# Re-planning the last stretch of a 145-step kernel: half ticks, fixed places, and an earlier fetch

## The chip, the cores and the metric

The kernel runs on one core of a Trainium2 chip. TensorE does matrix products and transposes, VectorE and ScalarE do element-wise work, GpSimd does a power and issues accumulating transfers, and SyncE issues almost all other transfers. The metric is the time of one execution in microseconds (us), as the median over runs.

## The reference

The input `x` has 32 images of 14 x 14 pixels and 512 channels, in float32. Two layers follow each other; both normalise in 32 groups of 16 channels first and both add their input back.

```python
for i in range(18):                                   # layer 0, on gn(x)
    nx = gelu(x @ block_w[i] + block_b[i])            # 512 x 512, every pixel
    if i in (11, 14, 17):
        h = gelu(nx.mean(pixels) @ fc1_w[t] + fc1_b[t])          # 512 -> 128
        gates = softmax((h @ fc2_w[t] + fc2_b[t]).reshape(B, 3, C), axis=1)
        nx = nx + gammas[t] * sum_a(gates[:, a] * anchor[a])     # anchors: x after 1, 4, 9
    x = nx
x = x_in + x                                          # end of layer 0
x = x + conv3x3(gn(x), W, groups=32)                  # layer 1
```

## The kernel before

**Layer 0.** The images are worked on in 8 pairs of tiles (pair 0 to 7; a tile is two images, so a pair is four). Channels lie on the 128 partitions in 4 chunks. One step is one block (`block`, L369) for one pair; 144 blocks and one gap step are interleaved in a written-out order (`steps`, L93 to L104), so that two pairs alternate and TensorE always has products. A block is seven products; after each of them the function `run` (L134) issues whatever stands in a calendar for that **tick**. A block thus has 7 ticks, of 8 matrix instructions (2.63 us) each. `tend` (L107) is the tick after the last block; this text calls it T, and writes T+3 for the third tick behind it. From T on there are no products: a tick is only what the calendar holds, and all engines work through their own queues in the order in which the calendar issues.

**The calendar.** `at` (L115) puts a function at a fixed tick. `put` (L124) looks for the first tick from a wished one on that has enough room left on VectorE ("dve") or ScalarE ("act"); the room of a tick is in `ROOM` (L111) for the blocks and in `TAIL` (L112) behind T. `hold` (L121) takes room away. Functions of one tick are issued in the order in which they were planned. So the calendar decides the order of instructions on each engine, not their times.

**The end of a pair.** After block 17, `plan_head` (L610) plans `gate_hidden` (L500: 4 products `hps` and a gelu), four `gate_base` (L564) on VectorE, `gate_logits` (L515: products `lps`) and `gate_softmax` (L525). `plan_gates` (L630) plans for each channel chunk `gate_part` (VectorE), `gate_last` (ScalarE) and `gate_add` (VectorE). `residual` (L662) adds the kernel's input to the result by an accumulating transfer from GpSimd's queue. `plan_norm` (L704) plans the statistics of layer 1's group norm: `stats`, then three steps `scales_mean` (L208: products `mps` and four small VectorE instructions), `scales_rstd` (L218: products `vps`, one VectorE instruction, a power on GpSimd) and `scales_newton` (L225: five VectorE instructions). `columns` (L669) then writes the un-normalised (e = 0) and normalised (e = 1) values in another order into `xc`, and two transfers from SyncE's queue put each `xc` into a DRAM buffer `x2d`, in runs of 56 numbers (224 bytes). For the last pair the chunks are planned one after the other, and e = 1 is made on VectorE; for the others on ScalarE.

**Layer 1** works in 4 batches of 8 images (two pairs each) and in 16 units per batch, four per channel chunk. `unit_load` (L811) fetches 448 KB from `x2d`; `unit_taps` (L828, tile `cps`) does 6 products, which the profile shows as 12 matrix instructions; `unit_sum` (L843) adds the taps to the un-normalised values on VectorE; `unit_out` (L850, tile `tpo`) transposes the sum on TensorE, and ScalarE copies it out. Every fourth unit a transfer of 784 KB takes a chunk to the output. `plan_unit` (L879) plans one unit. The first three batches fill gaps between blocks; the last six units of batch 2 ("late units", `NLATE` = 6) and all 16 units of batch 3 run behind T. Those 16 need both last pairs' `x2d`, chunk by chunk. There are 5 buffers for a unit's input.

`load_gates` (L471) fetches `fc1_w` (256 KB) and `fc2_w` (512 KB) for a gated block; SyncE's queue issues it in calendar order, between the other transfers.

Of the kernel before, what the change touches and what calls it, by code (L numbers as in the profile page):

```python
# [19 lines left out]
def kernel(  # L20
# [72 lines left out]
    steps = [(0, i) for i in range(12)]  # L93
# [12 lines left out]
    NP7 = 7  # L106
    tend = NP7 * len(steps)  # L107
# [1 line left out]


    ROOM = {"dve": (1.7, 0.0, 3.4, 3.4, 1.7, 0.0, 0.0), "act": (1.0, 0.8, 1.5, 1.5, 1.0, 0.8, 0.8)}  # L111
    TAIL = {"dve": 3.0, "act": 3.6}  # L112
    left = {e: {} for e in ROOM}

    def at(tick, fn, *args):  # L115
        calendar[tick].append((fn, args))

    def room(e, tick):
        return left[e].get(tick, ROOM[e][tick % NP7] if tick < tend else TAIL[e])

    def hold(e, tick, us):  # L121
        left[e][tick] = room(e, tick) - us

    def put(first, need, fn, *args):  # L124

        tick = first
        while any(room(e, tick) < us for e, us in need.items()):
            tick += 1
        for e, us in need.items():
            left[e][tick] = room(e, tick) - us  # L130
        at(tick, fn, *args)
        return tick
# [75 lines left out]
    def scales_mean(d, lo=0, hi=NR):  # L208
        st, mean, dv = d["st"][:, lo:hi], d["mr"][:, 0, lo:hi], d["dv"][:, lo:hi]
        ps = group_sums(f"mps_{d['name']}_{lo}", st[:, :, 1::3], hi - lo)  # L210
        nc.vector.tensor_scalar(mean, ps, 0.5, None, ALU.mult)
        nc.vector.tensor_tensor(
            dv, st[:, :, 1::3], mean.unsqueeze(2).to_broadcast([P, hi - lo, 2]), ALU.subtract
        )
        nc.vector.tensor_mul(dv, dv, dv)
        nc.vector.scalar_tensor_tensor(dv, dv, HW / 2.0, st[:, :, 2::3], ALU.mult, ALU.add)

    def scales_rstd(d, lo=0, hi=NR):  # L218

        ps = group_sums(f"vps_{d['name']}_{lo}", d["dv"][:, lo:hi], hi - lo)  # L220
        ve = d["ve"][:, lo:hi]
        nc.vector.tensor_scalar(ve, ps, 1.0 / HW, 1e-5, ALU.mult, ALU.add)
        nc.gpsimd.tensor_tensor(d["y"][:, lo:hi], ve, mhalf[:, lo:hi], ALU.pow)

    def scales_newton(d, lo=0, hi=NR):  # L225
        ve, y, e, mr = d["ve"][:, lo:hi], d["y"][:, lo:hi], d["e"][:, lo:hi], d["mr"]
        nc.vector.tensor_mul(e, y, y)
        nc.vector.tensor_mul(e, e, ve)
        nc.vector.tensor_scalar(e, e, -0.5, 1.5, ALU.mult, ALU.add)
        nc.vector.tensor_mul(mr[:, 1, lo:hi], y, e)  # L230
        nc.vector.scalar_tensor_tensor(
            mr[:, 2, lo:hi], mr[:, 0, lo:hi], -1.0, mr[:, 1, lo:hi], ALU.mult, ALU.mult
        )
# [376 lines left out]
    def plan_head(p, i):  # L610

        k = at_step[p, i]
        t1 = NP7 * (k + 1)
        name = f"{p}_{i}"
        ti = TARGETS.index(i)
        box = boxes[p, i] = {}
        end = k == len(steps) - 1
        if p == 0:
            at(t1 + 1, gate_differences, k, ti)
        at(t1 + (0 if end else 1), gate_hidden, k, ti, name, box)  # L620
        box["base"] = {
            (h, n): put(t1, {"dve": 1.0}, gate_base, p, i, h, n) for h in range(2) for n in range(2)
        }
        a = t1 + (1 if end else 2)
        while room("dve", a) < 2.2:
            a += 1
        at(a, gate_logits, k, name, box)
        return put(a, {"dve": 2.2}, gate_softmax, ti, name, box)
# [75 lines left out]
    def plan_norm(p, d, a, chunks):  # L704

        def stats(n, c, b):
            if "st" not in d:
                d.update(stats_tiles(f"b{p}"))  # L710
            stats_of(d, boxes[p, NB - 1]["nx"][c // NH][n][:, c % NH], c, n, (b,))

        last = a
        for c in chunks:
            for n in range(2):
                for b in range(NI):
                    last = max(last, put(a, {"dve": 0.36}, stats, n, c, b))
        r = chunks[0] * NB4, (chunks[-1] + 1) * NB4
        b = put(last + 1, {"dve": 0.8}, lambda: scales_mean(d, *r))
        b = put(b + 1, {"dve": 0.2}, lambda: scales_rstd(d, *r))  # L720
        b = put(b + 2, {"dve": 0.8}, lambda: scales_newton(d, *r))
        b += 1
        for c in chunks:
            for n in range(2):
                a = put(a, {"act": 0.6}, columns, p, c, n, d, 0)
        out = []
        for c in chunks:
            for n in range(2):
                for i in range(NI):
                    need = {"dve": 0.4} if p == NPAIR - 1 else {"act": 0.5}  # L730
                    b = put(b, need, columns, p, c, n, d, 1, (i,))
            out.append(b)
        return out
# [26 lines left out]
    UC = GP // 2  # L760
# [115 lines left out]

    done = []

    def plan_unit(m, u, tk, ahead, stay=False):  # L879
        b = tk - ahead  # L880
        if not stay and len(done) >= NBW:
            b = max(b, done[-NBW][0])
        if len(done) >= NX:
            b = max(b, done[-NX][1])
        at(b, unit_load, m, u)
        a = max(b + 2, tk)
        while room("dve", a + 1) < 0.65:
            a += 1
        at(a, unit_taps, m, u)
        b = put(a + 1, {"dve": 0.65}, unit_sum, m, u)  # L890
        b = put(b + 1, {"act": 0.9}, unit_out, m, u)
        done.append((a, b))

    def plan_batch(m):


        ready = [max(ended[p][c] for p in range(m * BP, (m + 1) * BP)) for c in range(NCK)]
        if m < NBAT - 1:
            t0 = ready[-1] + 6
            t1 = ended[(m + 2) * BP - 1][-1] if m < NBAT - 2 else NP7 * at_step[NPAIR - 1, GAP] - 9  # L900
            early = NU - (NLATE + NGAP if m == NBAT - 2 else 0)
            for u in range(early):
                plan_unit(m, u, t0 + (t1 - t0) * u // early, 8)
            if m == NBAT - 2:
                for j in range(NGAP):
                    tk = NP7 * at_step[NPAIR - 1, GAP] + NP7 * j // NGAP
                    hold("dve", tk + 1, -0.65)
                    hold("act", tk + 2, -0.9)
                    if j >= NBW:
                        at(tk - 10, load_bands, (early + j,))  # L910
                    plan_unit(m, early + j, tk, 10, j >= NBW)
                for j in range(NLATE):
                    left["dve"][tend + 1 + j] += 0.65
                    left["act"][tend + 2 + j] += 0.9
                    at(tend - 12 + j, load_bands, (early + NGAP + j,))
                    plan_unit(m, early + NGAP + j, tend + j, 12, True)
        else:
            at(tend - 7, load_bands, (0, 1), wpool, "w", [P, NCK, C])
            for j in range(2):
                at(tend - 8, load_bands, (2 + j,), cvpool, "bw")  # L920
            at(tend + 1, load_bands, (4, 5), wpool, "w", [P, NCK, C])
            tk = 0
            for u in range(NU):
                tk = max(tk + 1, ready[u // UC] + 3, tend + NLATE)
                plan_unit(m, u, tk, 3, True)


    for s in range(TS):
# [23 lines left out]
    NGAP, NLATE = 6, 6  # L952
    LEAD = 35
    for k in range(len(steps)):
        p, i = steps[k]
        if i == GAP:
            for tick in range(NP7 * k, NP7 * (k + 1)):
                left["dve"][tick], left["act"][tick] = 2.4, 2.2
            continue
        if k > 0:  # L960
            at(NP7 * (k - 1), load_block, k)
            for tk, j in ((4, 0), (4, 1), (4, 2), (5, 3)) if p == 0 else ((2, 1), (3, 0), (4, 2), (5, 3)):
                at(NP7 * (k - 1) + tk, sums, k, j)
            if p == 0:
                left["dve"][NP7 * (k - 1) + 4] = 0.0
        if i in TARGETS:
            at(NP7 * k + 4, load_gates, k)
            for tk, us in enumerate((0.8, 0.0, 1.5, 1.5, 0.5, 0.0, 0.0)):
                left["act"][NP7 * k + tk] = us
    for j in range(NLATE):  # L970
        left["dve"][tend + 1 + j] = TAIL["dve"] - 0.65
        left["act"][tend + 2 + j] = TAIL["act"] - 1.05
    for j in range(NLATE):
        left["dve"][tend + 1 + j] = TAIL["dve"] - 0.65
        left["act"][tend + 2 + j] = TAIL["act"] - 0.9
    left["act"][tend] = left["act"][tend + 1] = 0.0
    for j in range(NGAP):
        tk = NP7 * at_step[NPAIR - 1, GAP] + NP7 * j // NGAP
        hold("dve", tk + 1, 0.65)
# [14 lines left out]
    b = NP7  # L994
# [45 lines left out]
```

## Time and profile before

| what | value |
| --- | --- |
| median of 5 runs | 2996.19 us (2992.49 to 2999.58) |
| profiled execution, its own time | 2993.2 us |
| its span, first to last instruction | 2991.5 us |
| TensorE matmul busy | 2942.1 us, 98% of the span |
| VectorE busy | 1735.9 us, 58% |
| ScalarE busy | 1455.4 us, 49% |
| GpSimd busy | 77.5 us, 3% |
| moved by the transfers | 465.36 MB, mean 156 GB/s |

The profile is of one execution. Its rows give a start in us from the span's start, a length, the engine, the source line, the operation, and the tile written and the tiles read. A bracket at the end of a row gives idle time of the engine ahead of it and what ended that idle time. Engine names are PE (TensorE), DVE (VectorE), ACT (ScalarE), POOL (GpSimd) and SP (SyncE); a `q` behind a name is the engine's sequencer, which issues transfers. PEclk is the share of the full clock that TensorE was granted. TensorE's matrix instructions overlap, so a row's length is more than its share of the pace; the pace is read from the starts. When a transfer has landed is read from the semaphore updates that the trace records.

The products of the last block end at 2887.6 us in this execution. What lies behind that is the stretch from T on: 104 us, 3.5% of the span.

### The profile page before, as it was taken

Reading aid. Unit: us, or ns where it says so; the run is one execution under the profiler, and the core shown is the slowest. Engines: PE = TensorE matmul, PEld = TensorE weight load, DVE = VectorE, ACT = ScalarE, POOL = GpSimd, SP = SyncE. Lnnn points to the kernel's source line nnn. Section 1 sums busy time; section 2 is a strip of 40 time slices with the busy share of each in tenths; the row PEclk is TensorE's granted clock in tenths of the full one; section 3 lists DMA queues with packets and bytes.
Section 4 is the critical chain, followed back from the end, with each engine's and each line's share of the span. In section 5 each row is a group of like instructions: output and inputs, shape, how many; then the busy total and the mean of one; then the engine's idle time right before and its main releaser. Section 6 shows DMA issues by size and latency. Waiting matters only on the chain.

```text
span 2991.5 us, 31717 instructions
## 1 busy us (share of the span) xinstructions
PE 2942.1 (98%) x10073; PEld 1808.3 (60%) x10073; DVE 1735.9 (58%) x3317; ACT 1455.4 (49%) x3459; POOL 77.5 (3%) x60
## 2 busy tenths in 40 slices
PE   7999999999999999999999999999999999999996
PEld 4555555555565666666666666666666665656666
DVE  5877777655367454663546635566455663545663
ACT  3445445555455454554545544455445554444562
POOL 0000000000000000000000000000000000000010
PEclk9999999999999999999999999999999999999998
DMA  4444445644375445654456544556445653444689
GB/s 154 154 169 134 155 134 169 182 123 123 124 193 158 134 130 161 189 160 131 153 148 187 166 133 139 171 167 174 140 123 174 176 155 119 131 135 117 206 222 212
DMA packets 385743, 465.36 MB, mean 156 GB/s; under 512 B 150715, under 2 KB 213290, under 8 KB 385578
## 3 DMA queue, kind: packets, MB, share of 16 engines
q1 hardware_dynamic: 355178, 436.85, 48.0%
q0 software_dynamic: 4608, 12.85, 2.5%
q10 hardware_dynamic: 25792, 13.65, 1.7%
q8 instruction: 81, 1.33, 0.2%
q14 instruction: 84, 0.69, 0.1%
HBM read 381.48 MB, written 81.79 MB: 155 GB/s over the span
## 4 chain that ended last, share of the span: by engine, by line
PE 97%; DMA 1%; DVE 1%; issue 0%; POOL 0%; ACT 0%; SPq 0%; DVEq 0%
PE x L388 51%; PE z L388 25%; PE y L388 13%; PE cps L836 5%; PE lps L520 1%; PE tpo L860 1%; PE hps L504 1%; PE tpi L258 1%; DMA x<-x2d 0%; DMA w<-in_L_conv_block_w_dram 0%; DMA x2d<-xc 0%; DMA w<-in_L_conv_fc_w_dram 0%; DVE st_a L196 0%; PE mps_a L203 0%; DMA xin<-in_x_dram 0%; PE vps_a L203 0%
## 5 line engine op out<-in xcount | busy, mean ns | idle before, releaser
L388 PE MATMUL x<-t,s 128*128 128x392 f32 x2304 | 810.0, 494 | 0.0
L401 ACT ACTIVATE o<-c,bias 128x392 f32<-128x392 f32 x720 | 440.8, 620 | 661.2 <-DVE c L425 657.9
L388 PEld LDWEIGHTS x<-t,s 128*128 128x128 f32 x2304 | 432.5, 190 | 297.5
L425 DVE TENSOR_TENSOR c<-x,c 128x392 f32<-128x392 f32 x288 | 160.8, 565 | 516.3 <-PE x L388 424.5
L421 ACT COPY c<-x 128x392 f32<-128x392 f32 x576 | 278.9, 484 | 360.5 <-PE x L388 355.5
L388 PE MATMUL z<-t,s 128*128 128x392 f32 x1152 | 403.1, 493 | 0.0
L388 PE MATMUL x<-t,w 128*128 128x392 f32 x1152 | 403.0, 493 | 0.0
L388 PE MATMUL z<-o,s 128*128 128x392 f32 x1088 | 380.9, 493 | 0.0
L388 PE MATMUL y<-o,w 128*128 128x392 f32 x1088 | 380.5, 492 | 0.0
L388 PE MATMUL x<-o,w 128*128 128x392 f32 x1088 | 380.3, 492 | 0.0
L425 DVE TENSOR_TENSOR c<-y,c 128x392 f32<-128x392 f32 x288 | 163.0, 566 | 294.1 <-PE y L388 206.2
L388 PEld LDWEIGHTS x<-t,w 128*128 128x128 f32 x1152 | 217.9, 190 | 156.7
L388 PEld LDWEIGHTS z<-t,s 128*128 128x128 f32 x1152 | 217.0, 190 | 152.2
L367 DVE TENSOR_TENSOR t<-o,o 128x784 f32<-128x784 f32 x272 | 264.1, 971 | 65.4 <-ACT o L401 63.5
L388 PEld LDWEIGHTS x<-o,w 128*128 128x128 f32 x1088 | 206.4, 190 | 147.2
L388 PEld LDWEIGHTS y<-o,w 128*128 128x128 f32 x1088 | 205.1, 190 | 145.6
L388 PEld LDWEIGHTS z<-o,s 128*128 128x128 f32 x1088 | 205.0, 190 | 145.3
L367 DVE TENSOR_TENSOR t<-o,t 128x784 f32<-128x784 f32 x272 | 264.3, 972 | 4.7
L421 ACT COPY c<-z 128x392 f32<-128x392 f32 x288 | 139.5, 484 | 207.2 <-PE z L388 207.0
L425 DVE TENSOR_TENSOR c<-z,c 128x392 f32<-128x392 f32 x288 | 159.2, 564 | 119.0 <-PE z L388 118.1
L408 ACT ACTIVATE o<-c,bias 128x196 f32<-128x196 f32 x288 | 129.4, 450 | 91.2 <-DVE c L425 90.5
L401 ACT ACTIVATE o<-x,bias 128x392 f32<-128x392 f32 x240 | 137.6, 582 | 72.3 <-PE x L388 66.3
(104 smaller groups left out, 2052.1 us busy)
## 6 DMA issues: line engine op xcount, KB each, us to landing
w<-in_L_conv_block_w_dram SPq DMA_DIRECT2D x144, 1024.0 KB
s<-skeep SPq DMA_DIRECT2D x504, 256.0 KB
x2d<-xc SPq DMA_DIRECT2D x128, 224.0 KB
x<-x2d SPq DMA_DIRECT2D x64, 448.0 KB
skeep<-s SPq DMA_DIRECT2D x72, 256.0 KB
bw<-band SPq DMA_DIRECT2D x38, 384.0 KB
xkeep<-xt SPq DMA_DIRECT2D x32, 392.0 KB
o<-xkeep POOLq DMA_DIRECT2D x32, 392.0 KB, 7.6
```

The lines of the kernel that those rows point to most:

```text
L258: nc.tensor.transpose(tp[:, c * TP : (c + 1) * TP], xs[:, c * P : (c + 1) * P], ident[:TP, :TP])
L367: nc.vector.tensor_tensor(t[j], i0, i1, ALU.subtract)
L388: nc.tensor.matmul(acc[d][:, :N], lhsT=lhsT[:, kk, d * P : (d + 1) * P], rhs=rhs[:, kk, :], start=first and kk == 0, stop=kk == NH - 1, sk ...
L401: nc.scalar.activation(o[:, d, :], srcs[d], AF.Gelu_apprx_tanh, bias=bias[:, r : r + 1])
L408: nc.scalar.activation(o[:, d, sl], srcs[d][:, sl], AF.Gelu_apprx_tanh, bias=bias[:, r : r + 1], accum_out=pooled[:, c, m : m + 1],)
L421: nc.scalar.copy(cs[d], acc[d][:, :N])
L425: nc.vector.tensor_tensor(cs[d], acc[d][:, :N], cs[d], ALU.add)
L504: nc.tensor.matmul(hps[:, :NB4], lhsT=w1[:, kk, :], rhs=box["pooled"][:, kk, :], start=(kk == 0), stop=(kk == NCK - 1),)
L520: nc.tensor.matmul(lps[:, m * NB4 : (m + 1) * NB4], lhsT=w2[:, m * P : (m + 1) * P], rhs=h, start=True, stop=True,)
L836: nc.tensor.matmul(pv[:, :, lo:hi], lhsT=d["bw"][:, g, dy], rhs=xv[:, :, lo + dy - 1 : hi + dy - 1], start=j == 0, stop=j == 2, skip_group ...
L860: nc.tensor.transpose(tp[:NV, j * P : (j + 1) * P], d["xs"][:, g, 0, v * NV : (v + 1) * NV], ident)
```

## The change

All of it is in the planning; no instruction's work changes, but their order does.

- A tick behind T has half the room (`TAIL` 3.0 to 1.5 and 3.6 to 1.7).
- In the last head, `gate_logits` is fixed at T+1 and `gate_softmax` at T+3, behind one late unit's taps; before, the planner put both at T+2, behind two.
- The three steps of `plan_norm` go to fixed ticks, whether there is room or not; this holds for all pairs.
- The six late units and the 16 units of batch 3 stand at fixed places two ticks apart: taps at a, sum at a+1, out at a+2, and the next unit's taps at a+2 as well. Before, they were one tick apart and sum and out went where there was room.
- The last `load_gates` moves from tick 4 of the last block to tick 1.
- `unit_load` of batch 3 is planned up to 6 ticks ahead of the taps instead of 3.

```diff
-    TAIL = {"dve": 3.0, "act": 3.6}
+    TAIL = {"dve": 1.5, "act": 1.7}
...
-        a = t1 + (1 if end else 2)
+        if end:
+            at(t1 + 1, gate_logits, k, name, box)
+            at(t1 + 3, gate_softmax, ti, name, box)
+            return t1 + 4
+        a = t1 + 2
         while room("dve", a) < 2.2:
             a += 1
...
-        b = put(last + 1, {"dve": 0.8}, lambda: scales_mean(d, *r))
-        b = put(b + 1, {"dve": 0.2}, lambda: scales_rstd(d, *r))
-        b = put(b + 2, {"dve": 0.8}, lambda: scales_newton(d, *r))
-        b += 1
+        b = last + 1
+        for us, fn, step in (
+            (0.8, scales_mean, 1), (0.2, scales_rstd, 2), (0.8, scales_newton, 1)
+        ):
+            hold("dve", b, us)
+            at(b, fn, d, *r)
+            b += step
...
-    def plan_unit(m, u, tk, ahead, stay=False):
+    def plan_unit(m, u, tk, ahead, stay=False, fixed=False):
...
-        while room("dve", a + 1) < 0.65:
+        while not fixed and room("dve", a + 1) < 0.65:
             a += 1
         at(a, unit_taps, m, u)
-        b = put(a + 1, {"dve": 0.65}, unit_sum, m, u)
-        b = put(b + 1, {"act": 0.9}, unit_out, m, u)
+        if fixed:
+            b = a + 2
+            at(a + 1, unit_sum, m, u)
+            at(b, unit_out, m, u)
+        else:
+            b = put(a + 1, {"dve": 0.65}, unit_sum, m, u)
+            b = put(b + 1, {"act": 0.9}, unit_out, m, u)
         done.append((a, b))
...
                 for j in range(NLATE):
-                    left["dve"][tend + 1 + j] += 0.65
-                    left["act"][tend + 2 + j] += 0.9
                     at(tend - 12 + j, load_bands, (early + NGAP + j,))
-                    plan_unit(m, early + NGAP + j, tend + j, 12, True)
+                    plan_unit(m, early + NGAP + j, tend + 2 * j, 12 + j, True, True)
...
             for u in range(NU):
-                tk = max(tk + 1, ready[u // UC] + 3, tend + NLATE)
-                plan_unit(m, u, tk, 3, True)
+                tk = max(tk + 2, ready[u // UC] + 4, tend + 2 * NLATE)
+                plan_unit(m, u, tk, min(6, tk - ready[u // UC] - 1), True, True)
...
-            at(NP7 * k + 4, load_gates, k)
+            at(NP7 * k + (1 if k == len(steps) - 1 else 4), load_gates, k)
...
-    for j in range(NLATE):
-        left["dve"][tend + 1 + j] = TAIL["dve"] - 0.65
-        left["act"][tend + 2 + j] = TAIL["act"] - 1.05
-    for j in range(NLATE):
-        left["dve"][tend + 1 + j] = TAIL["dve"] - 0.65
-        left["act"][tend + 2 + j] = TAIL["act"] - 0.9
-    left["act"][tend] = left["act"][tend + 1] = 0.0
+        hold("dve", tend + 2 * j + 1, 0.65)
+        hold("act", tend + 2 * j + 2, 0.9)
+    hold("dve", tend, -0.6)
+    hold("dve", tend + 1, -0.3)
+    hold("dve", tend + 3, 0.85)
+    for tick in range(tend, tend + 4):
+        hold("act", tick, room("act", tick))
```

## The prediction, made before the changed kernel was run

> **What bounds the kernel now.** I read the page first.
>
> ```profile
> PE 2942.1 (98%) x10073; PEld 1808.3 (60%) x10073; DVE 1735.9 (58%) x3317; ACT 1455.4 (49%) x3459; POOL 77.5 (3%) x60
> ...
> PE 97%; DMA 1%; DVE 1%; issue 0%; POOL 0%; ACT 0%; SPq 0%; DVEq 0%
> ```
>
> TensorE is busy nearly throughout and carries 97% of the chain that ends last. Only a stretch where it idles can give time back. The view of its waits names such stretches:
>
> ```profile
> PE cps L836 <- DMA x<-x2d: 9.7, 2, 9.0
> ...
> PE hps L504 <- DMA w<-in_L_conv_fc_w_dram: 3.0, 1, 3.0
> ```
>
> Both stand behind T; its other waits are in the first 27 us or behind T too. Between, TensorE waits for nothing, so only a new wait could change the time there. TensorE's timeline behind T:
>
> ```profile
> 2890.63 1.49 PE L504 MATMUL hps<-pool,w 128*128 128x4 f32 x8 [3.04 <-DMA w<-in_L_conv_fc_w_dram]
> 2891.97 7.46 PE L836 MATMUL cps<-x,bq 128*128 128x224 f32 x24
> 2899.27 1.84 PE L520 MATMUL lps<-h,w 128*128 128x4 f32 x16
> ...
> 2938.91 4.05 PE L836 MATMUL cps<-x,bq 128*128 128x224 f32 x12 [9.00 <-DMA x<-x2d]
> ...
> 2978.06 2.33 PE L836 MATMUL cps<-x,bq 128*128 128x224 f32 x12
> 2980.22 0.60 PE L860 MATMUL tpo<-ident,x 128*112 128x128 f32 x4
> 2980.66 2.33 PE L836 MATMUL cps<-x,bq 128*128 128x224 f32 x12
> 2982.83 0.60 PE L860 MATMUL tpo<-ident,x 128*112 128x128 f32 x4
> 2983.80 0.62 PE L860 MATMUL tpo<-ident,x 128*112 128x128 f32 x4 [0.37 <-DVE x L846]
> ```
>
> It has two parts: head and norms until batch 3's unit 0 starts (I call this start S: 2938.91), then 16 units to the last `tpo` at 2983.80. In the second part TensorE is the bound: taps start every 2.60 us (2980.66 - 2978.06), because the `tpo` between two taps belongs to an earlier unit, whose sum is long made. What releases S stands in the chain of waits:
>
> ```profile
> 2929.67 5.03 DMA x2d<-xc
> 2934.77 4.09 DMA x<-x2d
> ```
>
> A write to `x2d` has to land, then the unit's load. SyncE's timeline tells why the write is that late:
>
> ```profile
> 2886.18 1.03 SPq L474 DMA_DIRECT2D w<-in_L_conv_fc_w_dram  x1
> ...
> 2909.11 21.77 SPq L697 DMA_DIRECT2D x2d<-xc  x14
> ```
>
> Chunk 0's normalised columns are done at 2923.6 (VectorE's row of 1.25 at 2922.39), but their writes are the last two of fourteen.
>
> **Part by part.** I placed the functions behind T by the planner's rules, by hand, and followed each engine's queue.
>
> *Earlier fetch.* It passes four `x2d` writes (SyncE's row at 2880.88), which start 1.6 us later (1.03 for `fc1_w`, 0.55 for `fc2_w`); their readers come over 40 us later, so this costs nothing. `hps` then waits for the last pooled gelu, whose ScalarE row ends at 2888.55, and starts near 2888.6 instead of 2890.63: -2.0. It would be 0 if the weights still came last; I take -2.0, since the issue moves from 2886.2 to about 2880.9 and issue to landing took 4.3.
>
> *Clock.* The view by stretches (PE, PEld, DVE, ACT, POOL busy, then granted clock, transfer share, GB/s):
>
> ```profile
> 2893.00:2899.00 6.00, 6.00 (x22) 5.76 (x21) 0.65 (x2) 0.00 (x0) 0.00 (x0) 0.60 1.08 265
> ...
> 2921.00:2931.00 10.00, 3.02 (x12) 2.79 (x12) 9.06 (x40) 2.24 (x5) 2.08 (x2) 0.50 1.32 212
> ```
>
> After 3.04 us idle the granted clock fell to 0.60, and the taps of two units took 7.46 where 4.5 is usual. With 1.0 us idle I take the full clock, since the stretch from 2901.5 to 2912, with a gap of 0.76, was granted 1.00: taps 2.2, `hps` 0.9. If it falls nevertheless, 2 to 3 us are lost here. [...]
>
> *Logits behind one unit.* 2888.6 + 0.9 `hps` + 2.2 taps + 1.8 `lps` = 2893.5, against 2901.1. From there the softmax took 2.7; ScalarE's tanh now stands behind a pair of copies (+0.3). Gates at 2896.6 against 2903.8: -7.2. VectorE is through with `gate_base` and the first sum by 2893.4. By the landing records the residuals came at 2895.4 to 2902.7, beside the same volume; chunk 0's first parts may wait 0 to 1.5 for them, taken as 0, because a late unit's sum is due in VectorE's queue at the same time.
>
> *Units two ticks apart.* Here the order turns against the change. At tick a+2 the calendar holds `unit_out` of unit u, planned first, then `unit_taps` of u+1. TensorE's queue goes taps u, `tpo` u, taps u+1, and `tpo` u waits for `unit_sum` u on VectorE. Behind the waiting `tpo` stand all later products, those of the norms too, and for these VectorE waits. The last unit before shows the price, as nothing lies between: taps at 2980.66, its `tpo` at 2983.80, which is 3.14, and 0.44 more (2980.66 - 2980.22) until next taps could start: 3.58 per unit against 2.60, so +0.98.
>
> *First norm.* Gates 2896.6 + 0.6 for a late unit's sum = 2897.2, its `tpo` at 2897.4. Then 0.44, two units of 3.58, and taps of 2.17 come before `mps`: 2907.2, the mean 0.5 later (2912.9 before). Mean to 2908.5, `vps`, `tpo`, the last late taps from 2909.7, their sum to 2912.7, newton 0.95, a `gate_add` 0.5, columns 1.25: 2915.4 against 2923.6, or -8.2.
>
> *Transfers to S.* Ahead of chunk 0's last two writes SyncE issues four others, the first of them when ScalarE has copied chunk 1's plain columns, about 2914.9; an output transfer starts a moment earlier. By the landing records a write beside an output landed 5.4 after its issue (3.1 alone), and each next one 1.3 to 1.4 later (2917.83, 2919.20, 2920.60, 2922.02). So 2914.9 + 5.4 + 5 x 1.35 = 2927.1, and 4.1 for the load: S = 2931.2, -7.7. Behind the load's issue stand eight more writes and two loads in SyncE's queue, so the chunks that follow find a backlog. Best for S: the two writes wait for nobody, 2915.4 + 0.6 + 3.1 + 4.1 = 2923.2; worst: as late as now. I lean to the middle, because from 2921 to 2931 the transfer engines were full (share 1.32) at only 212 GB/s.
>
> [...]
>
> *Sixteen units.* Fifteen hand-overs at +0.98: +14.7. `scales_rstd` of chunk 2 puts `vps`, one VectorE row and two `gate_part` between taps and sum of unit 2, 0.35 + 0.25 + 0.7 = 1.3; that of chunk 3 another 0.65 at unit 5: +1.95. The cold first unit (4.05) costs the same as now. Chunk edges: chunk 1's normalised columns stand behind unit 0's sum on VectorE; then come two writes, behind the backlog, and the load. I get waits of 0.7 at unit 4, 1.7 at unit 8 and none at 12, against 0.7 before (at 2951.93): +1.7. Bounds for an edge: 0, and 9.0, the longest such wait now.
>
> *Norm steps of pairs 0 to 6.* They move by up to 6 ticks, with columns and units behind them. `mps` now follows product Y, when the statistics are done (2871.7 against 2873.5 in the last block). So the products hide it: 0. Without that cover, nine small VectorE rows, 2 us, stand in TensorE's way for each of pairs 0 to 5: 12 us. Pair 6's newton passes in front of the last `gate_base` rows: 1 us, inside the 2893.4 above.
>
> Sum: -7.7 (all before S is in it) + 14.7 + 1.95 + 1.7 = +10.6, rounded to +10. The profiled execution's 2993.2 becomes 3003; it lay 3.0 under the median of 2996.2, so I say 3006.
>
> **Rivals.**
>
> (1) About even: S comes near its best and the chunk edges hide. S -12 to -15, hand-overs +14.7, rstd +1.95: +2 to +5. For it: writes of chunk 1 could slip through while SyncE would otherwise idle. Against: all six writes stand in one queue, 1.35 apart.
>
> (2) Faster: the hand-over costs only the 0.37 that the bracket of the last row shows. Place: each `tpo` from S on. 15 x 0.37 = 5.6, rstd 1.95, S at its best -15.7: -8. It decides if taps come under 3.0 apart; with that and S before 2926 the kernel is faster. Against: a pace is set by starts, and taps to `tpo` of one unit took 3.14 there.
>
> (3) Worse: the clock. Hand-overs leave TensorE idle for about a quarter; with a chunk edge inside, the clock falls as it did after 2887.6, for 2 to 3 us each, at two or three places: +15 to +18. Against: from 2912 to 2921 it was granted 0.85 with half of the time idle.
>
> **How the numbers follow.** My case (+6 to +14) has 0.58, (1) 0.22, (2) 0.07, (3) 0.13. About 0.2%, 6 us, is what a measurement of this kernel can tell from no change. Slower by more: 0.58 + 0.13 and 0.02 from (1)'s upper edge, 0.73; the same: 0.20; faster: 0.07. The range goes from 0 to +17, 2996 to 3013: all of my case and of (1), most of (3).
>
> **What would show it.** Right: `hps` near 2888.7; S between 2927 and 2934; the last taps 3.5 to 3.6 apart, each `tpo` with a wait for DVE `x` L846, over 5 us of such waits in the list (1.1 now); the last `tpo` near 2994. Wrong: taps 2.6 apart, S before 2924, a wait of TensorE between start-up and T, or over 8 us of `cps` waits for loads behind S.

## The result, and the profile after

| | before | after |
| --- | --- | --- |
| median | 2996.23 us (43 runs, 2992.44 to 3006.21) | 3002.39 us (22 runs, 3000.76 to 3005.73) |
| ratio after / before | | 1.0019, 95% interval 1.0013 to 1.0025 |
| profiled execution, its span | 2993.2, 2991.5 | 3002.26, 3000.6 |
| T, taken as the start of the last block's last matrix instruction | 2887.10 | 2887.03 |
| from T to the end of the span | 104.4 | 113.6 |
| from T to S (batch 3's unit 0 starts) | 51.8 | 43.6 |
| from S to the last `tpo` | 44.9 | 62.3 |

The change makes the kernel slower by 0.19%, about 6 us. T is equal in both profiles to 0.1 us, so the 9.1 us between the two profiled executions lie behind T, where the stretch is 9.2 longer: 8.2 won before S, 17.4 lost after it.

The page of after has the same busy times, and the chain that ended last the same shares. A 0.2% change does not show there:

```profile
PE 2941.5 (98%) x10073; PEld 1805.0 (60%) x10073; DVE 1736.4 (58%) x3317; ACT 1453.7 (48%) x3459; POOL 77.9 (3%) x60
...
PE 97%; DVE 1%; DMA 1%; issue 0%; POOL 0%; SPq 0%; ACT 0%; DVEq 0%
```

TensorE's waits behind T tell it (engine, tile and line, what it waited for: us in total, times, longest):

```profile
PE tpo L867 <- DVE x L853: 15.1, 18, 1.5
PE cps L843 <- DMA x<-x2d: 12.4, 1, 12.4
...
PE hps L504 <- ACT o L408: 0.4, 1, 0.4
```

The wait of `hps` for the weights (3.0) is gone. In its place stands the hand-over: 18 waits of a transposition for the sum that VectorE has yet to make, 15.1 us against 1.1 in the same list of before:

```profile
PE tpo L860 <- DVE x L846: 1.1, 2, 0.8
```

TensorE's timeline of after shows the two halves:

```profile
2888.52 0.39 PE L504 MATMUL hps<-pool,w 128*128 128x4 f32 x2 [0.36 <-ACT o L408]
2888.77 2.41 PE L843 MATMUL cps<-x,bq 128*128 128x224 f32 x12
2891.01 1.84 PE L520 MATMUL lps<-h,w 128*128 128x4 f32 x16
...
2930.60 4.63 PE L843 MATMUL cps<-x,bq 128*128 128x224 f32 x12 [12.39 <-DMA x<-x2d]
2935.95 1.10 PE L867 MATMUL tpo<-ident,x 128*112 128x128 f32 x4 [0.72 <-DVE x L853]
2936.85 3.60 PE L843 MATMUL cps<-x,bq 128*128 128x224 f32 x12
...
2986.17 2.33 PE L843 MATMUL cps<-x,bq 128*128 128x224 f32 x12
2989.30 0.62 PE L867 MATMUL tpo<-ident,x 128*112 128x128 f32 x4 [0.81 <-DVE x L853]
2989.76 2.33 PE L843 MATMUL cps<-x,bq 128*128 128x224 f32 x12
2992.90 0.62 PE L867 MATMUL tpo<-ident,x 128*112 128x128 f32 x4 [0.81 <-DVE x L853]
```

The logits end at 2892.8 instead of 2901.1, S comes at 2930.60 instead of 2938.91; then the starts of the taps are 3.59 apart (2989.76 - 2986.17) instead of 2.60. The chain that ended last has a new member, VectorE's sum, once per unit:

```profile
2921.59 4.96 DMA x2d<-xc
2926.60 3.96 DMA x<-x2d
2930.60 4.65 PE cps L843 x12
2935.27 0.63 DVE x L853
...
2989.93 2.18 PE cps L843 x12
2992.13 0.63 DVE x L853
2992.90 0.63 PE tpo L867 x4
```

### The profile page after: what moved, and what is told of

Read it like the earlier page. It is cut to its first block, busy times and chain, and to the rows that moved or that the text cites. A ratio compares the mean times of both kernels' runs of the same rounds, so it can differ in the third digit from the quotient of the medians.

```text
span 3000.6 us, 31734 instructions
## 1 busy us (share of the span) xinstructions
PE 2941.5 (98%) x10073; PEld 1805.0 (60%) x10073; DVE 1736.4 (58%) x3317; ACT 1453.7 (48%) x3459; POOL 77.9 (3%) x60
## 4 chain that ended last, share of the span: by engine, by line
PE 97%; DVE 1%; DMA 1%; issue 0%; POOL 0%; SPq 0%; ACT 0%; DVEq 0%
PE x L388 51%; PE z L388 25%; PE y L388 13%; PE cps L843 5%; PE lps L520 1%; PE tpo L867 1%; PE tpi L258 1%; PE hps L504 1%; DVE x L853 0%; DMA tw<-in_L_conv_W_dram 0%; DMA w<-in_L_conv_block_w_dram 0%; DMA x2d<-xc 0%; PE vps_b L203 0%; DVE st_a L196 0%; DMA x<-x2d 0%
```

## The experiments

T lies between 2885.7 us (experiment 10) and 2891.1 us (experiment 2) in the profiles, so places behind T are given from T. "Tail" is T to the end of the span. A ratio is to runs of before taken beside the version (one set each for after, for 1 to 4, 5 to 8, 9 to 11, and 12), whose medians lay between 2994.6 and 2996.9; medians of different sets compare to some 2 us only. Added lines shift the line numbers: L836, L843, L846 and L851 are the same taps, L860, L867, L870 and L875 the same transpositions.

| version | median, us | ratio to before, interval | S from T | tail |
| --- | --- | --- | --- | --- |
| before | 2996.23 | 1 | 51.8 | 104.4 |
| after | 3002.39 | 1.0019 (1.0013 to 1.0025) | 43.6 | 113.6 |
| 1 later hand-over, batch 3 | 2993.70 | 0.9989 (0.9980 to 0.9998) | 43.3 | 104.3 |
| 2 before, with the hand-over | 3010.38 | 1.0043 (1.0030 to 1.0057) | 51.8 | 120.9 |
| 3 late fetch | 3006.35 | 1.0036 (1.0024 to 1.0048) | 48.1 | 116.8 |
| 4 norm steps by room, pairs 0 to 6 | 3015.11 | 1.0057 (1.0043 to 1.0072) | 58.5 | 124.7 |
| 5 the same, pairs 0 to 5 | 3003.63 | 1.0029 (1.0018 to 1.0041) | 46.0 | 116.0 |
| 6 (1) with the units behind all norms | 2998.15 | 1.0010 (1.0001 to 1.0019) | 46.4 | 110.2 |
| 7 (6) with chunk 0's writes first | 3000.29 | 1.0013 (1.0004 to 1.0022) | 47.5 | 110.7 |
| 8 (6) with idle products | 2997.59 | 1.0009 (1.0000 to 1.0018) | 47.8 | 108.5 |
| 9 later hand-over, every unit | 2990.41 | 0.9983 (0.9974 to 0.9992) | 40.5 | 103.5 |
| 10 (9) with chunk 0's writes first | 2993.66 | 0.9992 (0.9983 to 1.0001) | 41.2 | 105.5 |
| 11 before, a second profile | 2997.45, one run | | 54.5 | 108.0 |
| 12 (10) with unit 15's load ahead | 2990.81 | 0.9979 (0.9970 to 0.9987) | 37.1 | 102.8 |

**1. The hand-over taken away in batch 3.** After, with `unit_out` one tick later, so that another unit's taps lie between a unit's own taps and its `tpo`:

```diff
-            b = a + 2
+            b = a + (3 if m == NBAT - 1 else 2)
```

> The changed kernel, but in batch 3 each unit's out stands one tick later (a+3), so TensorE's queue goes taps u+1 before tpo u; all else as changed. Hand-over theory (the price is that tpo u waits for its own sum ahead of the next taps): taps again 2.6 us apart wherever the input is there; of the 14.7 us some 2 to 4 come back as a wait at unit 4, whose input cannot land before about 2948 because chunk 1's columns stand behind unit 0's sum; S stays at 2930.6, the last tpo comes near 2980 instead of 2992.9. So 10 to 13 us below the changed kernel, about 2990, and 4 to 7 below the kernel before. Rival (transfers set the pace of the units, the hand-over only fills their time): waits for loads take the place of the waits for sums, and the time stays within 3 us of the changed kernel, about 3000 to 3002.

8.7 us less than after, and 2 less than before. TensorE's waits in this kernel:

```profile
PE cps L843 <- DMA x<-x2d: 18.4, 5, 12.5
...
PE tpo L867 <- DVE x L853: 3.6, 5, 1.0
```

The hand-over waits shrink from 15.1 to 3.6 (four of the late units, and the last unit), and taps are 2.60 apart again where no load is waited for. But units 3, 4, 8 and 12 now wait 1.98, 1.18, 1.11 and 1.66 for their loads, 5.9 us in all; these edges had been hidden, as at 3.59 per unit the loads kept up. The expectation had allowed 2 to 4 us of such waits, at unit 4 alone, so the gain falls short of the 10 to 13 expected.

**2. The hand-over put into the kernel before.** One edit in `plan_batch`, which spaces batch 3's units two ticks apart:

```diff
-                tk = max(tk + 1, ready[u // UC] + 3, tend + NLATE)
+                tk = max(tk + 2, ready[u // UC] + 3, tend + NLATE)
```

> The kernel before with one part of the change alone: batch 3's units two ticks apart instead of one, so that tpo u stands ahead of taps u+1. S stays near 2938.9. Hand-over theory: taps 3.58 apart, 15 x 0.98 = 14.7 minus the 0.7 wait at unit 4 that is hidden now: +14, about 3010. Rival (transfers set the pace): under +5.

14.5 us over before. S stands where it stood (51.8 from T), `tpo` waits 17 times for VectorE's `x`, and TensorE's timeline has the pace of after:

```profile
2958.11 2.33 PE L836 MATMUL cps<-x,bq 128*128 128x224 f32 x12
2961.25 0.62 PE L860 MATMUL tpo<-ident,x 128*112 128x128 f32 x4 [0.80 <-DVE x L846]
2961.70 2.33 PE L836 MATMUL cps<-x,bq 128*128 128x224 f32 x12
```

With experiment 1 this shows the cause of the loss from both sides: the spacing alone costs what the prediction gave it.

**3. The fetch back at its old tick.** After, with the last `load_gates` at tick 4:

```diff
-            at(NP7 * k + (1 if k == len(steps) - 1 else 4), load_gates, k)
+            at(NP7 * k + 4, load_gates, k)
```

> The changed kernel with the last gate weights fetched at tick 4 again. Theory (the head is in the chain up to S): hps starts near 2890.6 instead of 2888.5, the clock falls for the late units as it did before, and S comes 2 to 5 us later; the time is 2 to 5 us above the changed kernel, about 3005 to 3007. Rival (S is set by SyncE's queue and the transfers, whatever the head does): within 1 us of the changed kernel.

4.0 us over after. TensorE's timeline:

```profile
2891.41 1.03 PE L504 MATMUL hps<-pool,w 128*128 128x4 f32 x8 [3.16 <-DMA w<-in_L_conv_fc_w_dram]
2892.29 4.09 PE L843 MATMUL cps<-x,bq 128*128 128x224 f32 x12
```

The wait is back, and so are slow taps behind it (4.09 where after has 2.41; in before the two units behind this wait took 7.46, at a granted clock of 0.60). S comes 4.5 later from T. So up to S the fetch is worth 2.8 by the wait and 1.7 by the slower taps; of these 4.5 us the tail keeps 3.2, for a reason told below under *The clock*. The earlier fetch does not always come in time: in experiments 4 to 7 and 9, which have it, `hps` still waited 0.2 to 1.45 for its weights.

**4. The norm steps of pairs 0 to 6 placed by room again.** In `plan_norm`, for these pairs:

```diff
         for us, fn, step in (
             (0.8, scales_mean, 1), (0.2, scales_rstd, 2), (0.8, scales_newton, 1)
         ):
+            if p < NPAIR - 1:
+                b = put(b, {"dve": us}, fn, d, *r) + step
+                continue
```

> The changed kernel with the three norm steps of pairs 0 to 6 placed by room again, as before; the last pair's stay fixed. Theory (the products hide them): within 1 us of the changed kernel, and TensorE waits for nothing between start-up and T in both. Rival (the fixed steps hold up or free something in the blocks): 3 to 12 us either way.

12.7 us over after, where within 1 was expected. ScalarE's timeline names the pair:

```profile
2937.02 7.17 ACT L694 ACTIVATE xc<-o,mr_b 128x196 f32<-128x196 f32 x16 [6.64 <-DVE mr_b L231]
```

Pair 6's newton found room only late behind T, now that the room is halved, and was done at 2937.0; its 16 columns stand behind it, and S comes 15 us later. With half ticks, pair 6 needs its fixed places; what fixed places do with whole ticks was not run.

**5. The same for pairs 0 to 5 alone.** As in 4, with `p < NPAIR - 2`.

> The changed kernel with the norm steps of pairs 0 to 5 placed by room; those of pairs 6 and 7 stay fixed. This splits the run that did so for pairs 0 to 6 and lost 12.7 us. Theory: the loss there was pair 6's newton alone (it found no room behind T until some 50 us later, and pair 6's columns and the loads of batch 3 with it); the products hide the steps of pairs 0 to 5, so this kernel is within 1 to 2 us of the changed one, about 3002. Rival: the fixed steps in the blocks give time by themselves, and this kernel loses part of the 12.7, over 3 us.

1.2 us over after by the medians, 2.9 if each is taken against its own runs of before (9.0 and 6.2 over); the intervals overlap. So most of 4's loss was pair 6's. That the blocks hide these steps for pairs 0 to 5 is better read from TensorE's waits: in before and after there is none between 30 us and T, in experiment 4, with pairs 0 to 6 placed by room, one of 0.2 us for VectorE's `c`, and here all that the list from 2870 us on names are behind T. The profile's longer tail (116.0) has its source behind T: `hps` waited 1.45 for its weights there and the next taps took 3.72, where after has 0.36 and 2.41. Whether the steps' places made the weights later is not shown.

**6. Batch 3's units behind all norms.** Experiment 1 with unit 0's taps from T+34, two ticks apart, and each load planned a tick behind its chunk's columns:

```diff
-                tk = max(tk + 2, ready[u // UC] + 4, tend + 2 * NLATE)
-                plan_unit(m, u, tk, min(6, tk - ready[u // UC] - 1), True, True)
+                tk = max(tk + 2, tend + 34)
+                plan_unit(m, u, tk, tk - ready[u // UC] - 1, True, True)
```

> The kernel with the out one tick later (2993.7), and batch 3's taps from T+34 on with every load planned one tick behind its chunk: all norm steps and columns of chunks 1 to 3 now stand ahead of the first sum in VectorE's queue. Theory (the waits at units 3, 4, 8 and 12 come from columns queued behind sums): S stays near 2930 to 2932, taps 2.6 apart to the end without waits for loads, 5 to 8 us less, about 2986 to 2989. Rival (the transfers are full from S on, and pace the units whatever the order): waits for loads stay at 5 us and more behind S, and the time within 2 us of 2993.7.

4.4 us over experiment 1, a gain of 5 to 8 being expected. TensorE's timeline:

```profile
2932.35 7.54 PE L843 MATMUL cps<-x,bq 128*128 128x224 f32 x24
...
2948.32 4.11 PE L843 MATMUL cps<-x,bq 128*128 128x224 f32 x12 [2.79 <-DMA x<-x2d]
...
2956.42 4.63 PE L843 MATMUL cps<-x,bq 128*128 128x224 f32 x12 [3.55 <-DMA x<-x2d]
```

By the landing records unit 0's input was there at 2929.37, but its taps stood behind chunk 3's norm products. VectorE was through with chunk 1's columns at 2921.7; their writes stood behind others in SyncE's queue, the last landing at 2944.69, and unit 4's load went out at 2944.82. TensorE waited there and at unit 5, each time with slow taps behind it (4.11 and 4.63 instead of 2.4). So what holds these units up is no longer VectorE's order but the writes, one behind the other in SyncE's queue.

**7. Chunk 0's writes first.** Experiment 6 with pair 6's other columns planned behind pair 7's columns of chunk 0:

```diff
+    first = []
...
+                if p == NPAIR - 1 and first:
+                    a = max(a, first[0] + 1)
...
+                    if p == NPAIR - 2 and c > 0:
+                        b = max(b, first[0] + 1)
...
+        if p == NPAIR - 1:
+            first.append(b)
...
-    for tick in range(tend, tend + 4):
+    for tick in (tend, tend + 3):
         hold("act", tick, room("act", tick))
```

> As the kernel with the norms first, and pair 6's normalised columns of chunk 0 made at T+1 and T+2, its other chunks and chunk 1's plain columns behind pair 7's chunk 0: so the two writes that release unit 0 have no other write directly ahead of them. Theory (S is set by writes queued in SyncE's queue at 1.35 us each): S 4 to 6 us earlier, the time 4 to 6 us less than the kernel with the norms first. Rival (S is set by something else, the output transfer or the landing itself): within 2 us of it.

2.1 us over experiment 6. Unit 0's input landed at 2927.0, 39.2 from T against 43.4 there, so the edit did what it says; but the taps again stood behind the norm products (S at 2935.38), and the displaced writes kept unit 5 waiting 8.11 us.

**8. TensorE kept busy with idle products.** Experiment 6 with 24 products of no use to anyone at T+24:

```diff
+    def warm():
+        ps = aux("warm")
+        for j in range(24):
+            nc.tensor.matmul(ps[:, :P], lhsT=ident, rhs=gmask, start=True, stop=True)
+
+    at(tend + 24, warm)
```

> As the kernel with the norms first, with 24 products of two constant tiles, used for nothing, in TensorE's queue between the norms of chunks 2 and 3, to fill part of its wait before S; its output is otherwise untouched. Theory (the first two units take 4.6 and 3.6 instead of 2.33 because the clock fell in the wait): 1 to 3 us less than the kernel with the norms first, if the products end close enough to S. Rival: the clock falls anyway, or the products push the norms back: 0 to 3 us more.

0.6 us under experiment 6; the intervals overlap, so no difference is shown. TensorE's timeline:

```profile
2925.84 7.56 PE L909 MATMUL warm<-gmask,ident 128*128 128x128 f32 x48
...
2935.13 4.57 PE L843 MATMUL cps<-x,bq 128*128 128x224 f32 x24
```

The first two units' taps take 4.57 at a granted clock of 1.00 instead of experiment 6's 7.54 (in experiment 9 the first two took 7.26, at 0.62), so 3.0 us are there to be had from the clock; but the products took 7.56 and pushed chunk 3's norms, which then released S later (47.8 from T instead of 46.4), and unit 4 waited 3.97 for its load instead of 2.79.

**9. The later hand-over for the late units too.** After with one edit:

```diff
-            b = a + 2
+            b = a + 3
```

> The kernel after with every fixed unit handed over a tick later, so that the six late units too have another unit's taps between their own taps and their transposition. Hand-over theory: the late units come 2.6 us apart in place of 3.58, so chunk 0's mean and with it S come about 3 us earlier than in the version with the later hand-over in batch 3 alone (2993.7), and the time is 2 to 4 us under it, about 2990 to 2992. Rival, the writes of the columns and VectorE's other work set S: within 1.5 us of that version.

The mean of chunk 0 comes 16.6 from T instead of 19.8 in experiment 1, and S 40.5 instead of 43.3: 3.2 and 2.8 earlier, as the hand-over has it. TensorE's timeline has the late units 2.6 apart:

```profile
2897.06 2.33 PE L843 MATMUL cps<-x,bq 128*128 128x224 f32 x12
2899.23 0.60 PE L867 MATMUL tpo<-ident,x 128*112 128x128 f32 x4
2899.66 2.33 PE L843 MATMUL cps<-x,bq 128*128 128x224 f32 x12
```

The median is 3.3 under experiment 1; as the two ran against different runs of before and their intervals overlap, the profile carries this reading more than the times do. The interval against before lies wholly below 1: this version beats both kernels, before by 6 us and after by 12.

**10. Experiment 9 with chunk 0's writes first** (the edits of 7).

> The version before it with chunk 0's writes first: ScalarE's room for pair 6's columns opens a tick later, pair 6's columns of chunk 0 come first and its others, with chunk 1's columns of the other pairs, stand behind pair 7's columns of chunk 0. Theory: x of unit 0 lands about 4 us earlier, as it did where chunk 0's writes came first before, and TensorE is free to take it, so the time is 2 to 4 us under the version before it. Rival: the later units' loads find the same writes ahead of them, and the time is within 1.5 us of it or above it.

3.3 us over experiment 9. TensorE's timeline, at late unit 15 and at unit 0:

```profile
2907.69 4.64 PE L851 MATMUL cps<-x,bq 128*128 128x224 f32 x12 [3.87 <-DMA x<-x2d]
...
2926.95 6.57 PE L851 MATMUL cps<-x,bq 128*128 128x224 f32 x24 [7.72 <-DMA x<-x2d]
```

Pair 6's two writes of chunk 0 now stood ahead of unit 15's load in SyncE's queue. The load landed 21.9 from T (18.4 in 9), unit 15's sum waited for it, and newton and chunk 0's columns, behind that sum in VectorE's queue, began 5.7 later from T. From the start of these columns to unit 0's input it was 12.7 instead of 17.6, so the two nearly cancel. Behind S, units 3 and 4 waited 2.48 and 4.43 for their loads (0.58 and 2.46 in 9), as the rival has it.

**11. Before, profiled again**, to see where its spread of 14 us sits.

> The kernel before, profiled once more. If its spread between runs lies in the start-up and the blocks ahead of the tail, the tail from T takes 104.4 us again, within 1 us; if it lies in the tail (clock and transfers), the tail differs by 2 to 10 us.

The tail took 108.0, 3.6 more. TensorE's timeline in this profile, and SyncE's:

```profile
2893.98 1.84 PE L504 MATMUL hps<-pool,w 128*128 128x4 f32 x8 [5.79 <-DMA w<-in_L_conv_fc_w_dram]
```

```profile
2887.25 1.25 SPq L474 DMA_DIRECT2D w<-in_L_conv_fc_w_dram  x1
2888.54 0.54 SPq L479 DMA_DIRECT2D w<-w2keep  x1
```

The weights were issued 0.45 before T, against 0.92 before it in the first profile, and by the landing records took 6.60 instead of 4.32; the wait was 5.79 instead of 3.04. So of the 3.6 us between these two profiles 2.75 are this wait; how much of the spread over all runs it makes, two profiles do not show.

**12. Experiment 10 with unit 15's load ahead of chunk 0's writes**: ScalarE's room closed up to T+3 as in 9, and unit 10 alone handed over at a+2.

```diff
-            b = a + 3
+            b = a + (2 if a == tend else 3)
...
-    for tick in (tend, tend + 3):
+    for tick in range(tend, tend + 4):
```

> The version with every unit's hand-over a tick later and chunk 0's writes first, where now unit 15's load stands ahead of chunk 0's writes in SyncE's queue: ScalarE's room stays closed until T+3, so pair 6's columns of chunk 0 are made behind it, and unit 10 alone is handed over at the earlier tick, where the logits lie between its taps and its transposition. In the version before it that load stood behind two writes, landed 22 us behind T, and held VectorE up ahead of newton for 5.7 us. Theory, this one load ate the gain of the earlier writes: unit 15 waits under 1 us, chunk 0's normalised columns are done 23 to 24 us behind T, x of unit 0 lands 36 to 38 us behind T (40.4 and 41.2 in the two versions before), and the time is 2 to 4 us under the version with the later hand-over alone (2990.4), about 2987 to 2988. Rival, the loads of the later units then find the same writes ahead of them: x of unit 0 earlier, but longer waits at units 4 to 8, and the time within 1.5 us of 2990.4 or above it.

Each step came as expected up to S: unit 15 did not wait, chunk 0's columns were done 23.6 from T, S at 37.1. The time is within 0.4 us of experiment 9 and the intervals overlap, as the rival has it. TensorE's timeline, then the chain that ended last:

```profile
2938.74 0.60 PE L875 MATMUL tpo<-ident,x 128*112 128x128 f32 x4
2945.78 4.58 PE L851 MATMUL cps<-x,bq 128*128 128x224 f32 x12 [6.43 <-DMA x<-x2d]
```

```profile
2936.24 5.89 DMA x2d<-xc
2942.27 3.37 DMA x<-x2d
```

Unit 4's taps wait 6.43 for a load that waits for chunk 1's last write, issued at 2936.24 as the last of four, and the clock falls once more: 0.52 from 2945.8 to 2950.4, with these taps at 4.58. What is won at S is lost at chunk 1's edge.

## Why the prediction was right, and what was mis-sized

The forecast was 3006 with slower at 0.73; it is 3002.4 and slower. The mechanism stood: S earlier, then a hand-over per unit that costs more than S gives. Step by step, in the profiles:

| term | forecast | measured |
| --- | --- | --- |
| `hps` | starts near 2888.6 | from 2887.36, its last two at 2888.52 |
| gates ready | 2896.6 | 2895.9 |
| chunk 0's mean | 2907.7 | 2906.84 |
| chunk 0's columns done | 2915.4 | 2914.2 |
| write landed, then S | 2927.1, 2931.2 | 2926.55, 2930.60 |
| before S, against before | -7.7 | -8.2 |
| 15 hand-overs | +14.7 | +14.85 (15 x 3.59 against 15 x 2.60) |
| rstd at units 2 and 5 | +1.95 | +1.5 (4.67 and 4.00 against 3.59) |
| chunk edges | +1.7 | -0.9 (before: 3.49 against 2.60; after: none) |
| cold clock behind S | 0 | +2.3 (2.66 + 1.27, before 1.64) |
| other starts | 0 | -0.4 |
| sum | +10.6 | +9.2 |

*The edges.* The forecast put waits of 0.7 and 1.7 at units 4 and 8 on top of the hand-overs. There were none: the load of unit 4 landed at 2947.83, 2.1 ahead of its taps (2949.91), that of unit 8 at 2962.69, 1.9 ahead (2964.62). So this term was too large, and the 0.9 that before loses at its unit 4 is won. The hand-overs hide most of the edges, as experiment 1 shows, where they come back without it (5.9 us at four units). The rest of the slack is due to the next term: the taps came 2.3 later than forecast because of the clock. In experiment 3, where they came 1.3 earlier, unit 4 did wait, 0.26.

*The clock.* "The cold first unit (4.05) costs the same as now" was wrong; a unit is called cold when its taps take far more than the usual 2.33 to 2.43. Two units ran cold (4.63 and 3.60) where before had one (4.05). Two views by stretches, before S and behind it (PE, PEld, DVE, ACT, POOL busy, then granted clock, transfer share, GB/s):

```profile
2921.00:2930.60 9.60, 0.00 (x0) 0.00 (x0) 0.53 (x3) 0.20 (x1) 0.00 (x0) 0.50 1.13 205
2930.60:2939.40 8.80, 8.08 (x24) 7.17 (x25) 2.39 (x7) 0.59 (x2) 0.00 (x0) 0.50 1.29 220
```

The clock was granted at 0.50 up to 2939.4, through unit 0 and most of unit 1. With it the starts of units 1 and 2 came 6.25 and 4.86 behind their predecessors instead of 3.59 (before, unit 1 came 4.24 behind instead of 2.60). Why it was two is not shown. The wait ahead of S was 12.4 instead of 9.0, and the hand-over's wait followed at once; but experiment 3 has the same wait and the same hand-over, and only its unit 0 was cold. Its TensorE timeline at units 0, 1 and 4:

```profile
2935.87 4.63 PE L843 MATMUL cps<-x,bq 128*128 128x224 f32 x12 [12.35 <-DMA x<-x2d]
2941.70 2.33 PE L843 MATMUL cps<-x,bq 128*128 128x224 f32 x12
2953.91 2.43 PE L843 MATMUL cps<-x,bq 128*128 128x224 f32 x12 [0.26 <-DMA x<-x2d]
```

So 1.3 us of this term come or go from profile to profile, and experiment 3's tail regains them behind S.

*From the profile to the median.* The forecast moved the profiled 2993.2 to the median by adding 3.0. The profiles differ by 9.1, the medians by 6.2: the change also takes away part of before's spread (14 us against 5), most of which lies above the profiled execution. Experiment 11's profile, with a tail of 108.0, would have given +5.6. So the base of the sum was a favourable execution of before, and the loss was carried over in full. The profiles' +9.1 lies in the middle of the forecast's own case (+6 to +14), the medians' +6.2 at its lower edge. The 6 us that the forecast took for the least that can be told from no change were too many: the measured interval is some 4 us wide.

*The transfers' price.* Six writes of 224-byte runs landed 12.35 us behind the first one's issue (2914.20 to 2926.55), 1.24 apart; the sum had 12.15. So the price that the sum took from the landing records of before held to 0.2 us, and S came at 2930.60 where 2931.2 was forecast.

*The rivals.* "About even" (+2 to +5) would have needed S at 2924 to 2927 and hidden edges: the second came true, the first did not. "Faster" needed taps under 3.0 apart: they were 3.59. "Worse, by the clock" came true behind S, for 2.3 more than the sum had, not at two or three places.

*The unmoved part.* Between start-up and T there is no new wait of TensorE in after, and one of 0.2 us in experiment 4, with the norm steps of pairs 0 to 6 placed by room, so their 0 holds. The prediction did not see that the half ticks need pair 6's fixed steps (experiment 4).

What stays open: whether experiment 9 gains on experiment 1 by exactly the late units' hand-over, since the two were not run side by side; how much of before's spread the fetch makes; and what decides whether one unit behind S runs cold or two. A version that writes chunk 1 from another queue than SyncE's was not run.

## What to carry to other kernels

When a schedule is spread out, look at what stands directly behind a consumer that waits for another engine: here one transposition per unit, in front of the next unit's products, cost 0.99 us fifteen times, and one unit's products placed in between took it away (3002.4 to 2990.4 with a single number changed). Before adding a wait for a load to a slower pace, check whether the pace hides it. And where a stretch ends in a burst of small transfers, winning at its first consumer can only move the wait to the next one: the three versions here that changed the order of the writes (7, 10 and 12) did so, and no order that avoids it was found.

## What the runs showed of the hardware that was not expected

In these runs the clock did not fall at one fixed length of idle time. In experiment 9 TensorE idled 2.46 us before unit 4 and 2.45 us before unit 12; this is its timeline:

```profile
2945.91 2.43 PE L843 MATMUL cps<-x,bq 128*128 128x224 f32 x12 [2.46 <-DMA x<-x2d]
...
2971.49 4.11 PE L843 MATMUL cps<-x,bq 128*128 128x224 f32 x12 [2.45 <-DMA x<-x2d]
```

and its stretches around unit 12:

```profile
2968.50:2971.50 3.00, 0.55 (x6) 0.31 (x4) 0.62 (x1) 0.59 (x2) 0.00 (x0) 1.00 1.03 352
2971.50:2975.50 4.00, 4.00 (x13) 3.79 (x14) 0.00 (x0) 0.00 (x0) 0.00 (x0) 0.57 0.30 110
```

The first gap left the taps at 2.43, which before's unit 4 took at a granted clock of 1.00 (2952 to 2962). The second was followed by a granted clock of 0.57 from 2971.5 to 2975.5 and by taps of 4.11, 1.7 us more. Shorter gaps were followed by slow taps as well: in experiment 1 the taps behind a gap of 1.98 took 3.41, and in experiment 5 the taps behind a gap of 1.45 and the short `hps` took 3.72. So no length of gap separates the two cases in these runs. The waits named here, from 1.45 to 6.43 us, cost nothing or 1.0 to 2.2 us on top (1.0 in experiment 1, 1.3 in 5, 1.7 here, 2.2 in experiment 12), and such a wait is to be priced with that chance. The prediction's sum had nothing for this; its rival (3) had 2 to 3 us for each place.
